# Loads by output chunk, borrowed banks and a one-level first group in the opening of a two-layer recurrent kernel

## The chip, the cores and the metric

The kernel runs on one core of one Trainium2 chip. The metric is the device time of one execution in microseconds (us), taken as the median of several runs. Beside the times there is a profile of one execution. TensorE (PE) does the matmuls, VectorE (DVE), ScalarE (ACT) and GpSimd (POOL) the elementwise work. SyncE (SP) and ScalarE issue most of the DMAs; each engine works its instructions off strictly in the order in which the program gives them.

## The reference, cut to what matters

There are 128 sequences of 128 steps with 512 features, all in float32, and two recurrent layers one behind the other, each with a residual sum.

```python
def _L0_cond_ref(h_t, z, W, b, alpha):
    Wh = W[:, :D]
    Wz = W[:, D:]
    leak = 1.0 - alpha
    def step(h, z_t):
        gate = jax.nn.sigmoid(h @ Wh.T + z_t @ Wz.T + b)
        h_new = jnp.tanh(h * leak + gate * z_t)
        return (h_new, h_new)
    ...
def _L1_cond_ref(x, h0, Wx, Wh, b):
    xw = jnp.einsum('ntd,dh->nth', x, Wx) + b
    def step(prev_h, xw_t):
        next_h = jnp.tanh(xw_t + prev_h @ Wh)
        return (next_h, next_h)
    ...
x = x + _L0_cond_ref(cond_1024, x, ...)
x = x + _L1_cond_ref(x, cond_1024, ...)
```

Per layer and step there are two 512x512 products: of the input, which does not depend on the state, and of the state, which does. Both layers start from cond.

## The kernel before

Features lie on the 128 partitions, in four chunks (C = 4), and the 128 sequences along the free dimension. A 512x512 weight is a 4x4 arrangement of 128x128 blocks, so a *state product* (`state_product`, L437) is 16 matmuls of 128 columns: two halves of eight, each with its own PSUM bank, `r0a` and `r1a` for layer 0, `r0b` and `r1b` for layer 1.

**Groups and products.** Four steps (G = 4) form a group, held in a tile T of the `ring`. Instead of 64 block products per group, the input side is computed by a scheme of seven products numbered 1 to 7, in the order 1, 2, 6, 5, 7, 3, 4 (`OUTER`), of sums of inputs and differences of weights (`wc`). `multiply` has two forms. With *one level* (L345) a product is four matmuls of 256 columns; only layer 0's group 1 uses it. With *two levels* (L351) each of the seven is split once more into seven matmuls of 128 columns, which need nested differences of weights (`raw`: tiles wra, wrb; `nested`: wna, wnb), more sums of inputs (tiles R and N beside S), a `gather` at the end, and a second seed (`seed_second`, L430) for each bank. The products accumulate in two sets of PSUM banks, A and B; ACT copies three of them aside (`keep`, L362), VectorE adds others (`add`, L375).

**Step.** Layer 0's group 0 gets its input side directly: `input_product` (L450), 16 matmuls per step into the bank of that step. From step 4 on, ACT writes the group's result into the bank as a seed (L425). Then the state product, on ACT a sigmoid (`gate0`, L478), on VectorE the mix (`mix0`, L484 and L487), on ACT a tanh (`tanh0`, L492), and on POOL the residual sum (L496). The bank of a step is free for the next step once the mix has read it. Layer 1 (`tanh1`, L505) runs LAG = 9 steps behind, so its state products begin in step 9.

**Loads.** `load_x` loads one step of x (256 KB) in four DMAs of 64 KB, `load_w0` one half of layer 0's weight (wz or wh) in four of 256 KB, `load_w1` Wx or Wh of layer 1 likewise. The loads arrive with sequences or output features on the partitions; VectorE turns them in 32x32 blocks (`prepare_x`, `transpose_w0`), for Wx and Wh of layer 1 ACT permutes them (`permute_w1`, L206). The x tiles have five buffers. DMAs of SP and ACT share eight semaphores in turn, so a load waits on its queue until the load eight places earlier has landed.

**Order.** The order is written by hand. Each piece of work is entered in a list with a planned time (`at(time, fn, ...)`), the list is sorted, and the order of each engine follows from it. `shares(t)` says which products follow the state products of step t; `start[t]` is the planned begin of step t. These times only sort; nothing waits for a clock.

In the first steps, TensorE's order is: 24 warm-up matmuls on zeros (L172, L174), the input product of step 0, group 1's products 1, 2, 6, 5, 7, 3, state product 0, input product 1, state product 1, input product 2, state product 2, input product 3, product 4 of group 1, state product 3, and then layer 0's group 2 and layer 1's group 0 by one to three products a step, up to the end of step 8.

Of the kernel before, what the change touches and what calls it, by code (L numbers as in the profile page):

```python
# [13 lines left out]
def kernel(  # L14
# [64 lines left out]

    def cost(layer, g):  # L80
        return PRODUCT if (layer, g) == ("a", 1) else DEEP
# [3 lines left out]
    def shares(t):  # L85

        g, k = divmod(t, G)
        if t < 2 * G:
            return {
                2: [(0, 1, OUTER[6:])], 3: [(0, 2, OUTER[:2])], 4: [(0, 2, OUTER[2:4])],  # L90
                5: [(0, 2, OUTER[4:6])], 6: [(0, 2, OUTER[6:]), (1, 0, OUTER[:1])], 7: [(1, 0, OUTER[1:4])],
            }.get(t, [])
        if g == NG - 1:
            said = (
                [(1, g - 2, OUTER[4:])], [(1, g - 1, OUTER[:2])],
                [(1, g - 1, OUTER[2:4])], [(1, g - 1, OUTER[4:])],
            )[k]
        elif t >= T:
            said = [(1, NG - 1, ((1,), (2, 6), (5,), (3,), (7,), (4,))[t - T])] if t < T + 6 else []
        else:  # L100
            said = (
                [(1, g - 2, OUTER[4:])], [(0, g + 1, OUTER[:4])],
                [(0, g + 1, OUTER[4:])], [(1, g - 1, OUTER[:4])],
            )[k]
        return [x for x in said if 0 <= x[1] < NG]

    start, clock = [], 26.0
    for t in range(T + LAG + 4):
        start.append(clock)
        layers = (t < T) + (t >= LAG)  # L110
        busy = STATE * layers + (STATE + 0.6 if t < G - 1 else 0.0)
        for layer, g, which in shares(t):
            busy += cost("ab"[layer], g) * len(which)
        clock += max(busy, STATE + (3.0 if t < T else 0.7))
# [20 lines left out]
    def load_w0(h, name):  # L135
        view = w0.rearrange("(a i) (h q r) -> h q i a r", i=S, h=2, q=Q)[h]
        tile_ = tpool.tile([P, C, G, P], F32, tag="T", name=f"{name}_in")
        w_in[name] = tile_.rearrange("p a m r -> p (a m) r")
        for q in range(Q):
            both[q % 2].dma_start(out=w_in[name][q * S : (q + 1) * S], in_=view[q])  # L140
# [16 lines left out]
    def load_small():  # L157
        nc.gpsimd.memset(condT, 0.0)
        nc.gpsimd.memset(rows, 0.0)
        for i, v in enumerate((b0, alpha, b1)):  # L160
            nc.gpsimd.dma_start(
                out=rows[: Q * C, i], in_=v.rearrange("(a j) -> a j", j=S)
            )
        cond_view = cond.rearrange("(a i) (q r) -> q i a r", i=S, q=Q)
        for q in range(Q):
            nc.gpsimd.dma_start(out=cond_in[q * S : (q + 1) * S], in_=cond_view[q])

    def warm_up():

        ps = [L1.state_bank(-1, half) for half in range(2)]  # L170
        for n in range(12):
            nc.tensor.matmul(ps[n % 2][:, 0, : P // 2], condT[:, n % C], condT[:, 0, : P // 2], start=True, stop=True)  # L172
        for n in range(12):
            nc.tensor.matmul(  # L174
                ps[n % 2].rearrange("p m b -> p (m b)"), condT[:, 0], condT[:, 0:2].rearrange("p c b -> p (c b)"),
                start=True, stop=True,
            )
# [21 lines left out]
    def transpose_w0(w_T, name, kc):  # L199
        nc.vector.transpose(  # L200
            w_T[:, kc].rearrange("p m (q i) -> p m q i", i=S),
            w_in[name].rearrange("p (q m) (c j) -> p c m q j", q=Q, j=S)[:, kc],
        )
# [45 lines left out]
    class Layer:  # L249
# [87 lines left out]
        def multiply(self, g, outer, tag, first):  # L337
            if first:
                sets[tag] = psum.tile([P, 8, P], F32, tag=tag, name=f"{tag}_{self.name}_{g}_{outer}")
            if (self.name, g) == ("a", 1):  # L340
                ps = sets[tag][:, 0:4].rearrange("p (m h) b -> p m (h b)", m=2)
                a, w = self.left(g, outer), self.right(outer)
                for m in range(2):
                    for c in range(2):
                        nc.tensor.matmul(  # L345
                            ps[:, m], w[:, c, m, :], a[:, c],
                            start=first and m == 0 and c == 0, stop=c == 1, skip_group_check=True,
                        )
                return
# [6 lines left out]
        def places(self, g):  # L356
            return slice(0, 4 if (self.name, g) == ("a", 1) else 7)
# [49 lines left out]
        def terms(self, t, half):  # L407
# [3 lines left out]
            if (self.name, g) == ("a", 1):  # L411
                return (c[:, k % H : 4 : H],)
# [4 lines left out]
        def state_bank(self, t, half):  # L417
            self.state[t, half] = psum.tile(
                [P, 2, P], F32, tag=f"r{half}{self.name}", name=f"r{half}{self.name}_{t}"
            )  # L420
            return self.state[t, half]
# [20 lines left out]
        def input_product(self, t):  # L442

            g, k = divmod(t, G)
            ps = [self.state_bank(t, half) for half in range(2)]
            order = [(c, m) for c in range(C) for m in range(C)]
            if t > 0:
                order.sort(key=lambda p: (p[1] // 2, p[0], p[1]))
            for c, m in order:
                nc.tensor.matmul(  # L450
                    ps[m // 2][:, m % 2], self.w[:, c, m, :], ring[g][:, c, k],
                    start=c == 0 and m % 2 == 0, stop=False, skip_group_check=True,
                )
# [60 lines left out]
    at(0.1, load_w0, 1, "wz")  # L514
    at(0.11, warm_up)
    at(0.2, load_x, 0, both)
    for n, t in enumerate((4, 5, 6, 7)):
        at(0.3 + 0.01 * n, load_x, t, (both[t % 2],))
    at(0.4, load_w0, 0, "wh0")
    at(0.5, load_x, 1)  # L520
    at(12.5, small_vectors)
    at(9.5, prepare_x, 0)
    at(9.51, load_x, 2)
    for kc in range(C):
        at(10.0 + 0.6 * kc, transpose_w0, L0.w, "wz", kc)
    at(11.9, L0.input_product, 0)
    for t, time in ((4, 12.6), (5, 13.3), (6, 14.7), (7, 15.4)):
        at(time, prepare_x, t)
    for i, time in ((5, 14.0), (6, 16.1), (7, 16.8), (4, 17.5)):
        at(time, L0.combine_weights, i, nc.vector)  # L530
    for i, time in ((5, 16.2), (6, 17.4), (3, 18.7), (7, 20.0)):
        at(time, L0.add_up, 1, i, nc.gpsimd)
    L0.products(1, OUTER[:1], 14.4)
    L0.products(1, OUTER[1:6], 17.4)
    at(18.2, from_natural, condT, cond_in)
    for kc in range(C):
        at(18.9 + 0.6 * kc, transpose_w0, L0.wh, "wh0", kc)
    at(start[0] + 1.0, prepare_x, 1)
    at(start[0] + 1.01, load_x, 3)
    at(start[0] + 1.02, load_w1, wx1, "wx")  # L540
    at(start[0] + 1.03, load_w1, wh1, "wh1")
    at(start[1] + 0.05, prepare_x, 2)
    at(start[2] + 0.05, prepare_x, 3)
    for kc in range(C):
        at(start[1] + 2.5 + 0.1 * kc, permute_w1, L1.w, "wx", kc)
        at(start[5] + 0.1 + 0.4 * kc, permute_w1, L1.wh, "wh1", kc)
    for n, i in enumerate((5, 6, 7, 4)):
        at(start[0] + 5.1 + 0.01 * n, L0.combine_raw, i, nc.vector)
        at(start[0] + n, L0.combine_nested, i, nc.gpsimd)
        at(start[1] + 3.0 + n, L1.combine_weights, i, nc.gpsimd)  # L550
        at(start[3] + 5.6 + 0.01 * n, L1.combine_nested, i, nc.gpsimd)
        at(start[3] + 5.7 + 0.01 * n, L1.combine_raw, i, nc.gpsimd)

    for n, i in enumerate((5, 6, 3, 7)):
        at(start[2] + 2.0 + 0.1 * n, L0.add_up, 2, i, nc.gpsimd)
        at(start[2] + 6.0 + 0.01 * n, L0.add_up_raw, 2, 0, i, nc.vector)
        at(start[3] + (2.6, 2.61, 4.4, 4.41)[n], L0.add_up_nested, 2, "56", i, nc.vector)
        at(start[4] + 4.4 + 0.1 * n, L0.add_up_nested, 2, "73", i, nc.vector)
        at(start[2] + 6.1 + 0.01 * n, L0.add_up_raw, 2, 1, i, nc.vector)
        at(start[5] + 5.7 + 0.01 * n, L1.add_up, 0, i, nc.gpsimd)  # L560
        at(start[6] + (2.6, 2.61, 4.4, 4.41)[n] - 0.2, L1.add_up_raw, 0, 0, i, nc.vector)
        at(start[7] + (2.6, 2.61, 4.4, 4.41)[n], L1.add_up_nested, 0, "56", i, nc.vector)
        at(start[8] + 0.1 + 0.1 * n, L1.add_up_nested, 0, "73", i, nc.vector)
        at(start[8] + (2.9, 2.91, 4.9, 4.91)[n], L1.add_up_raw, 0, 1, i, nc.vector)
# [11 lines left out]
    for t in range(T + LAG):  # L576
        g, k = divmod(t, G)
        now = start[t]
        if AHEAD <= t + AHEAD < T:
            at((now, start[0] + 0.1, start[0] + 3.0, start[1] + 1.5)[t] if t < G else now + 0.01, load_x, t + AHEAD)  # L580
        if t < T:
            for i in range(2):
# [5 lines left out]
                if G <= t + 1 < T:  # L588
                    at(end + 1.85, L0.seed, t + 1, i)
                    at(now + 6.5, L0.seed_second, t + 1, i)  # L590
            at(end + 1.8, residual, t, h0)
            now += STATE
        if t < G - 1:
            at(now + 0.6, L0.input_product, t + 1)
# [27 lines left out]
        if t < G:  # L622
            at((start[1] + 0.1, start[1] + 0.2, start[2] + 0.1, start[2] + 0.2)[t], prepare_x, t + AHEAD)
        elif t + AHEAD < T:
            at(start[t + 1] + 6.4, prepare_x, t + AHEAD)
        if k == G - 1 and 2 <= g + 1 < NG:
            at(start[t] - 0.9, L0.gather, g + 1, 0, nc.vector)
            at(start[t + 1] - 0.9, L0.gather, g + 1, 1, nc.vector)
        if k == 1 and 0 <= g - 2 < NG - 2:
# [54 lines left out]
```

## Time and profile before

| | |
|---|---|
| median of 3 runs | 1656.34 us (1655.55 to 1657.14) |
| profiled execution, its own time | 1655.27 us |
| its span | 1653.3 us |
| mean granted TensorE clock | 0.998 |
| DMA moved | 73.99 MB, mean 45 GB/s |

In the page's 40 equal slices of the span, the share of the 16 DMA engines is 0.8 in the first, 0.2 in the second and at most 0.3 after that; VectorE is at 0.5 in the first, 0.6 in the second and 0.7 to 0.8 from then on until the last.

Lines of the profile begin with a time from the span's start where they are of a timeline, then the duration, engine, line of the source, operation, output tile <- input tiles, shape and count. A bracket gives the idle time before it and what ended it. A matmul of float32 appears as two records, so "x16" of 128x128 is eight matmuls. A matmul's duration includes a part that overlaps the next, so its price in a row of them is the distance from start to start. PE is the matmul, PEld the weight load.

### The profile page before, as it was taken

How to read it: one execution, taken by the hardware profiler on the slowest of the kernel's cores; microseconds unless marked ns; L12 is line 12 of the kernel's file. 1: busy time of each engine (PE TensorE's matmuls, PEld its weight loads, DVE VectorE, ACT ScalarE, POOL GpSimd, SP SyncE). 2: the span in 40 equal slices, each digit the busy share in tenths (PEclk: the TensorE clock that was granted, in tenths of full speed). 3: DMA queues.
4: the chain of work that ended last, by engine and by line, in shares of the span. 5: the costliest groups of instructions: out<-in, count | busy, mean ns of one | idle time of the engine just before them, and what ended most of it. 6: DMA issues, size and time to landing. Idle time of an engine off the chain costs nothing.

```text
span 1653.3 us, 37130 instructions
## 1 busy us (share of the span) xinstructions
PE 1638.3 (99%) x14500; PEld 1631.6 (99%) x14500; DVE 1324.0 (80%) x2978; ACT 793.4 (48%) x2046; POOL 665.7 (40%) x540
## 2 busy tenths in 40 slices
PE   9999999999999999999999999999999999999998
PEld 8989999999999999999999999999999999999998
DVE  5688788888888887888888888888888888888784
ACT  1444454544554444545445544445454454444454
POOL 4633443343344334334433433343344334333442
PEclk9999999999999999999999999999999999999999
DMA  8201211121122112111211211121112111211113
GB/s 171 53 9 40 46 45 40 40 49 42 39 46 46 40 40 47 44 40 41 50 40 39 46 46 40 39 48 43 40 42 49 39 40 44 48 39 27 27 21 64
DMA packets 153231, 73.99 MB, mean 45 GB/s; under 512 B 16801, under 2 KB 151969, under 8 KB 153057
## 3 DMA queue, kind: packets, MB, share of 16 engines
q1 hardware_dynamic: 148992, 69.53, 19.0%
q10 hardware_dynamic: 3840, 1.84, 0.6%
q8 instruction: 113, 1.85, 0.5%
q14 instruction: 62, 0.50, 0.1%
q0 software_dynamic: 224, 0.27, 0.1%
HBM read 38.02 MB, written 33.55 MB: 43 GB/s over the span
## 4 chain that ended last, share of the span: by engine, by line
PE 93%; DVE 2%; DMA 1%; POOL 1%; ACT 1%; issue 1%; SPq 0%; ACTq 0%; DVEq 0%; POOLq 0%
PE r0b L437 13%; PE r0a L437 13%; PE r1b L437 13%; PE r1a L437 13%; PE B_b L351 12%; PE A_a L351 11%; PE A_b L351 9%; PE B_a L351 8%; DMA x<-in_x_dram 1%; POOL T L496 0%; DVE h L487 0%; PE A_a L345 0%; POOL S_a L226 0%; POOL wcb L236 0%; DVE cb L375 0%
## 5 line engine op out<-in xcount | busy, mean ns | idle before, releaser
L496 POOL TENSOR_TENSOR T<-T,h 128x512 f32<-128x512 f32 x255 | 325.4, 1276 | 956.2 <-ACT h L492 888.9
L437 PE MATMUL r0a<-h,wha 128*128 128x128 f32 x2032 | 247.9, 275 | 0.0
L437 PE MATMUL r0b<-h,whb 128*128 128x128 f32 x2032 | 247.9, 275 | 0.0
L437 PE MATMUL r1a<-h,wha 128*128 128x128 f32 x2032 | 247.7, 275 | 0.0
L437 PE MATMUL r1b<-h,whb 128*128 128x128 f32 x2032 | 247.7, 275 | 0.0
L492 ACT ACTIVATE h<-h 128x256 f32<-128x256 f32 x256 | 106.7, 417 | 278.6 <-DVE h L487 273.0
L437 PEld LDWEIGHTS r0a<-h,wha 128*128 128x128 f32 x2032 | 237.3, 192 | 0.2 <-ACT h L492 0.2
L437 PEld LDWEIGHTS r0b<-h,whb 128*128 128x128 f32 x2032 | 237.1, 192 | 0.1
L437 PEld LDWEIGHTS r1a<-h,wha 128*128 128x128 f32 x2032 | 237.1, 192 | 0.0
L437 PEld LDWEIGHTS r1b<-h,whb 128*128 128x128 f32 x2032 | 237.1, 192 | 0.0
L478 ACT ACTIVATE r0a<-r0a,per_feature 128x128 f32<-128x128 f32 x256 | 87.6, 342 | 105.1 <-PE r0a L437 101.0
L484 DVE TENSOR_TENSOR r0a<-r0a,T 128x256 f32<-128x256 f32 x128 | 54.9, 429 | 89.7 <-ACT r0a L478 89.7
L484 DVE TENSOR_TENSOR r1a<-r1a,T 128x256 f32<-128x256 f32 x128 | 55.3, 432 | 65.6 <-ACT r1a L478 65.6
L189 DVE STREAM_TRANSPOSE T<-x 128x512 f32<-128x512 f32 x128 | 86.7, 681 | 12.7 <-DMA x<-in_x_dram 11.7
L194 DVE STREAM_TRANSPOSE o<-T 128x512 f32<-128x512 f32 x128 | 90.2, 705 | 4.1 <-POOL T L496 3.6
L478 ACT ACTIVATE r1a<-r1a,per_feature 128x128 f32<-128x128 f32 x256 | 85.3, 333 | 4.2
L226 POOL TENSOR_TENSOR S_a<-T 128x512 f32<-128x512 f32 x62 | 79.9, 1289 | 14.0 <-DVE T L189 14.0
L505 ACT ACTIVATE h<-r1b,per_feature 128x128 f32<-128x128 f32 x256 | 80.8, 370 | 8.5 <-PE r1b L437 6.3
L505 ACT ACTIVATE h<-r0b,per_feature 128x128 f32<-128x128 f32 x256 | 78.1, 355 | 11.2 <-PE r0b L437 10.3
L226 POOL TENSOR_TENSOR S_b<-T 128x512 f32<-128x512 f32 x64 | 82.5, 1289 | 0.1
L487 DVE SCALAR_TENSOR_TENSOR h<-h,leak,r0a 128x128 f32<-128x128 f32 x254 | 77.0, 345 | 5.3
L487 DVE SCALAR_TENSOR_TENSOR h<-h,leak,r1a 128x128 f32<-128x128 f32 x254 | 77.0, 345 | 4.5
(204 smaller groups left out, 3712.9 us busy)
## 6 DMA issues: line engine op xcount, KB each, us to landing
out_dram<-o SPq DMA_DIRECT2D x510, 64.0 KB, 1.8
x<-in_x_dram SPq DMA_DIRECT2D x502, 64.0 KB, 2.5
wx_in<-in_L_cond_Wx_dram SPq DMA_DIRECT2D x4, 256.0 KB, 5.3
wh_in<-in_L_cond_Wh_dram SPq DMA_DIRECT2D x4, 256.0 KB, 8.3
x<-in_x_dram ACTq DMA_DIRECT2D x10, 64.0 KB, 3.9
wz_in<-in_L_cond_W_dram ACTq DMA_DIRECT2D x2, 256.0 KB, 6.2
wz_in<-in_L_cond_W_dram SPq DMA_DIRECT2D x2, 256.0 KB, 5.6
wh_in<-in_L_cond_W_dram ACTq DMA_DIRECT2D x2, 256.0 KB, 5.9
```

Source lines behind the costliest of these rows:

```text
L189: nc.vector.transpose(dst.rearrange("p c (a i) -> p c a i", i=S), src.rearrange("p a (c j) -> p c a j", j=S))
L194: nc.vector.transpose(dst.rearrange("p a (c j) -> p c a j", j=S), src.rearrange("p c (a i) -> p c a i", i=S))
L226: eng.tensor_tensor(out(which), one(), two(), op)
L351: nc.tensor.matmul(sets[tag][:, n], self.right(outer, i), self.left(g, outer, i), start=first and n % 4 == 0, stop=True, skip_group_check= ...
L437: nc.tensor.matmul(ps[:, m], self.wh[:, c, 2 * half + m, :], h[t - 1][:, c], start=alone and n == 0, stop=c == C - 1, skip_group_check=True,)
L478: nc.scalar.activation(gate[:, m], gate[:, m], AF.Sigmoid, bias=per_feature[:, 0, f : f + 1])
L484: nc.vector.tensor_tensor(gate, gate, at_of(t)[:, two[i]], ALU.mult)
L487: nc.vector.scalar_tensor_tensor(h0[t][:, f], h0[t - 1][:, f], leak[:, f : f + 1], gate[:, m], ALU.mult, ALU.add)
L492: nc.scalar.activation(h0[t][:, two[i]], h0[t][:, two[i]], AF.Tanh)
L496: (eng or nc.gpsimd).tensor_tensor(at_of(t)[:, part], at_of(t)[:, part], h[t][:, part], ALU.add)
L505: nc.scalar.activation(h1[t][:, f], ps[:, m], AF.Tanh, bias=per_feature[:, 2, f : f + 1])
```

## The change

- `FLAT`: layer 1's group 0 also goes by one level, so it has no R and N sums, no second seeds and no gather.
- `load_w0` can load by output chunk: wz comes as four chunks of four 64 KB DMAs, and is turned in eight half-size transposes (per input chunk, first output half, then second).
- The loads are in the order x_0, wz by chunk, x_1, x_4, x_5, x_6, x_7, wh, cond, x_2, x_3, x_8 to x_11, Wx, Wh; up to cond all go on SP and ACT alternately. cond leaves POOL's queue.
- `input_product` is entered by halves. Steps 1 and 3 of layer 0 use layer 1's banks (`r0b`, `r1b`). Input product 1 follows input product 0; input product 2 stands after state product 0 and product 4 of group 1; input product 3 after state product 1.
- `shares` gives product 4 of group 1 to step 0 and two products each to steps 2 to 8.
- Ten wide warm-up matmuls (256 columns) instead of twelve of 64 and twelve of 256 columns.
- Group 1's first two sums move from POOL to VectorE, the small vectors move behind wh and cond, layer 0's raw differences before the first mix. x_3 and x_8 to x_11 are turned between the mixes of steps 0 and 1, followed by the first two sums of group 2. Layer 1's raw and nested differences come later on POOL; the copies of Wx and Wh come later on ACT.

From about step 10 on, the instructions of each engine are the same in both programs. Cut to its core:

```diff
+    FLAT = ("a", 1), ("b", 0)
+
     def cost(layer, g):
-        return PRODUCT if (layer, g) == ("a", 1) else DEEP
+        return PRODUCT if (layer, g) in FLAT else DEEP
...
-        if t < 2 * G:
+        if t <= 2 * G:
             return {
-                2: [(0, 1, OUTER[6:])], 3: [(0, 2, OUTER[:2])], 4: [(0, 2, OUTER[2:4])],
-                5: [(0, 2, OUTER[4:6])], 6: [(0, 2, OUTER[6:]), (1, 0, OUTER[:1])], 7: [(1, 0, OUTER[1:4])],
+                0: [(0, 1, OUTER[6:])], 2: [(0, 2, OUTER[:2])], 3: [(0, 2, OUTER[2:4])], 4: [(0, 2, OUTER[4:6])],
+                5: [(0, 2, OUTER[6:]), (1, 0, OUTER[:1])], 6: [(1, 0, OUTER[1:3])], 7: [(1, 0, OUTER[3:5])],
+                8: [(1, 0, OUTER[5:])],
             }.get(t, [])
...
-    def load_w0(h, name):
+    def load_w0(h, name, chunks=None):
...
+        for m in (None,) if chunks is None else chunks:
+            rows_ = slice(None) if m is None else slice(m, None, C)
+            for q in range(Q):
+                both[q % 2].dma_start(out=w_in[name][q * S : (q + 1) * S, rows_], in_=view[q][:, rows_])
...
+    def load_cond():
         cond_view = cond.rearrange("(a i) (q r) -> q i a r", i=S, q=Q)
         for q in range(Q):
-            nc.gpsimd.dma_start(out=cond_in[q * S : (q + 1) * S], in_=cond_view[q])
+            both[q % 2].dma_start(out=cond_in[q * S : (q + 1) * S], in_=cond_view[q])
...
-        for n in range(12):
-            nc.tensor.matmul(ps[n % 2][:, 0, : P // 2], condT[:, n % C], condT[:, 0, : P // 2], start=True, stop=True)
-        for n in range(12):
+        for n in range(10):
...
         def state_bank(self, t, half):
...
+            tag = "b" if self.name == "a" and t in (1, 3) else self.name
+            self.state[t, half] = psum.tile([P, 2, P], F32, tag=f"r{half}{tag}", name=f"r{half}{self.name}_{t}")
...
-        def input_product(self, t):
+        def input_product(self, t, half):
...
     at(0.0, load_small)
-    at(0.1, load_w0, 1, "wz")
-    at(0.11, warm_up)
-    at(0.2, load_x, 0, both)
-    for n, t in enumerate((4, 5, 6, 7)):
-        at(0.3 + 0.01 * n, load_x, t, (both[t % 2],))
-    at(0.4, load_w0, 0, "wh0")
-    at(0.5, load_x, 1)
-    at(12.5, small_vectors)
-    at(9.5, prepare_x, 0)
-    at(9.51, load_x, 2)
+    at(0.01, warm_up)
+    at(0.1, load_x, 0, both)
+    at(0.2, load_w0, 1, "wz", range(C))
+    for n, t in enumerate((1, 4, 5, 6)):
+        at(0.4 + 0.1 * n, load_x, t, both)
+    at(3.6, prepare_x, 0)
+    at(3.7, load_x, 7, both)
+    at(3.8, load_w0, 0, "wh0")
+    at(4.0, load_cond)
     for kc in range(C):
-        at(10.0 + 0.6 * kc, transpose_w0, L0.w, "wz", kc)
-    at(11.9, L0.input_product, 0)
+        at(6.0 + 0.4 * kc, transpose_w0, L0.w, "wz", kc, two[0])
+        at(8.6 + 0.4 * kc, transpose_w0, L0.w, "wz", kc, two[1])
+    at(7.7, L0.input_product, 0, 0)
+    at(9.9, L0.input_product, 0, 1)
+    at(10.3, prepare_x, 1)
+    at(10.31, load_x, 2)
+    at(11.8, L0.input_product, 1, 0)
+    at(13.6, L0.input_product, 1, 1)
...
-    for i, time in ((5, 16.2), (6, 17.4), (3, 18.7), (7, 20.0)):
-        at(time, L0.add_up, 1, i, nc.gpsimd)
-    L0.products(1, OUTER[:1], 14.4)
-    L0.products(1, OUTER[1:6], 17.4)
-    at(18.2, from_natural, condT, cond_in)
+    for i, time, eng in ((5, 16.5, nc.vector), (6, 17.2, nc.vector), (3, 17.9, nc.gpsimd), (7, 18.0, nc.gpsimd)):
+        at(time, L0.add_up, 1, i, eng)
+    L0.products(1, OUTER[:6], 15.4)
     for kc in range(C):
-        at(18.9 + 0.6 * kc, transpose_w0, L0.wh, "wh0", kc)
+        at(20.5 + 0.6 * kc, transpose_w0, L0.wh, "wh0", kc)
+    at(23.0, from_natural, condT, cond_in)
+    at(23.01, small_vectors)
+    for half in range(2):
+        at(start[0] + STATE + PRODUCT + 0.1 + 1.8 * half, L0.input_product, 2, half)
+        at(start[1] + STATE + 0.1 + 1.8 * half, L0.input_product, 3, half)
+    at(start[0] - 1.0, prepare_x, 2)
+    at(start[0] + 5.5, prepare_x, 3)
+    at(start[0] - 0.5, load_w1, wx1, "wx")
+    at(start[0] + 8.8, load_w1, wh1, "wh1")
...
-        at(start[0] + 5.1 + 0.01 * n, L0.combine_raw, i, nc.vector)
+        at(start[0] + 0.2 + 0.01 * n, L0.combine_raw, i, nc.vector)
...
-        at(start[5] + 5.7 + 0.01 * n, L1.add_up, 0, i, nc.gpsimd)
-        at(start[6] + (2.6, 2.61, 4.4, 4.41)[n] - 0.2, L1.add_up_raw, 0, 0, i, nc.vector)
-        at(start[7] + (2.6, 2.61, 4.4, 4.41)[n], L1.add_up_nested, 0, "56", i, nc.vector)
-        at(start[8] + 0.1 + 0.1 * n, L1.add_up_nested, 0, "73", i, nc.vector)
-        at(start[8] + (2.9, 2.91, 4.9, 4.91)[n], L1.add_up_raw, 0, 1, i, nc.vector)
+        at(start[0] + 9.6 + 0.1 * n, L0.add_up, 2, i, (nc.vector, nc.gpsimd)[n // 2])
...
+        at(start[4] + 4.4 + 0.01 * n, L1.add_up, 0, i, nc.gpsimd)
...
-        if t < G - 1:
-            at(now + 0.6, L0.input_product, t + 1)
+        if t == 1:
             now += STATE
...
-            at((start[1] + 0.1, start[1] + 0.2, start[2] + 0.1, start[2] + 0.2)[t], prepare_x, t + AHEAD)
+            at(start[0] + (6.2, 6.9, 8.0, 9.5)[t], prepare_x, t + AHEAD)
...
-        if k == 1 and 0 <= g - 2 < NG - 2:
+        if k == 1 and 1 <= g - 2 < NG - 2:
```

## The prediction

> **What bounds the kernel now.** I read the page first: busy times and the chain that ended last.
>
> ```profile
> PE 1638.3 (99%) x14500; PEld 1631.6 (99%) x14500; DVE 1324.0 (80%) x2978; ACT 793.4 (48%) x2046; POOL 665.7 (40%) x540
> PE 93%; DVE 2%; DMA 1%; POOL 1%; ACT 1%; issue 1%; SPq 0%; ACTq 0%; DVEq 0%; POOLq 0%
> ```
>
> TensorE is the bound, so only matmul work added or removed, and TensorE's idle or half-speed time, can move the end. Next, the table by stage, cut where TensorE starts its first real product (13.25), step 0 (31.18), group 2's first product (61.23), layer 1's first product (83.12), step 9 (105.78) and step 10 (120.68). Columns: length, then busy time of PE, PEld, DVE, ACT, POOL, then granted clock, DMA share, GB/s.
>
> ```profile
> 0.00:13.25 13.25, 11.92 (x49) 10.87 (x49) 2.59 (x5) 0.00 (x0) 4.67 (x13) 1.00 0.93 160
> 13.25:31.18 17.93, 15.89 (x82) 13.79 (x81) 12.81 (x22) 4.32 (x5) 10.99 (x8) 0.90 0.74 157
> 31.18:61.23 30.05, 28.32 (x233) 26.97 (x232) 18.77 (x45) 9.54 (x25) 13.84 (x11) 1.00 0.62 135
> 61.23:83.12 21.89, 21.89 (x196) 21.73 (x195) 15.09 (x34) 13.61 (x35) 16.76 (x18) 1.00 0.05 13
> 83.12:105.78 22.66, 19.67 (x164) 18.61 (x163) 19.65 (x44) 9.83 (x23) 7.17 (x6) 1.00 0.05 13
> 105.78:120.68 14.90, 13.91 (x123) 13.56 (x122) 13.38 (x28) 7.56 (x19) 7.08 (x6) 1.00 0.01 1
> 120.68:1653.00 1532.32, 1526.66 (x13666) 1526.08 (x13664) 1241.72 (x2806) 748.53 (x1940) 605.22 (x480) 1.00 0.19 42
> ```
>
> The last row has nothing to gain, and from about step 10 on the two programs have the same instructions. The prediction is therefore about when TensorE reaches step 9, 105.78 now. TensorE's timeline gives the prices and the stall:
>
> ```profile
> 9.17 0.79 PE L174 MATMUL r1b_-1_112<-condT 128*128 128x256 f32 x2
> 9.80 0.59 PE L174 MATMUL r0b_-1_111<-condT 128*128 128x256 f32 x2
> 16.82 1.89 PE L345 MATMUL A_a<-T,wa 128*128 128x256 f32 x8
> 18.55 1.89 PE L345 MATMUL B_a<-T,wa 128*128 128x256 f32 x8
> 22.48 3.10 PE L345 MATMUL A_a<-S_a,wca 128*128 128x256 f32 x8 [2.04 <-POOL S_a L226]
> 25.37 2.51 PE L345 MATMUL B_a<-S_a,wca 128*128 128x256 f32 x8
> ```
>
> From start to start a one-level product takes 1.73 us (16.82 to 18.55), a state or input product 3.57 (16 pairs), a two-level product 1.56 (61.23 to 62.79). Product 6 of group 1 waits 2.04 us for POOL's sums, and then products run at half clock: 22.48 to 31.18 is 8.70 for 4 x 1.73 = 6.92.
>
> Lost time per stage (length less work): 13.25 to 31.18, 17.93 - (3.57 + 6 x 1.73) = 4.0; to 61.23, 30.05 - (7 x 3.57 + 1.73 for steps 0 to 3, three input products and product 4) = 3.3; to 83.12, 21.89 - (7 x 1.56 + 3 x 3.57) = 0.3; to 105.78, 22.66 - (7 x 1.56 + 2 x 3.57) = 4.6; to 120.68, 14.90 - (2 x 3.57 + 4 x 1.56) = 1.5. The waits of TensorE (total, times, longest) name part of it:
>
> ```profile
> PE B_b L351 <- DVE R_b L226: 1.6, 2, 0.9
> PE r0b L437 <- DVE r0b L430: 0.9, 1, 0.9
> PE B_b L351 <- DVE cb L375: 0.7, 1, 0.7
> PE r1a L450 <- DVE h L487: 0.9, 2, 0.7
> ```
>
> Layer 1's two-level group 0 waits for its sums (R_b), its additions (cb) and its second seeds; the input products of steps 1 to 3 wait until the mix (h) frees their bank.
>
> **The loads.** Now x_7 lands at about 17.7 (VectorE turns it and x_6 from 17.75). The changed program needs x_0, wz, x_1, x_4 to x_7 by then: 40 loads of 64 KB, 2.62 MB. The nearest rows are two stages with both queues loading, 2:10 and 10:15, and one with SP alone (same columns):
>
> ```profile
> 2.00:10.00 8.00, 8.00 (x32) 7.35 (x32) 0.00 (x0) 0.00 (x0) 3.51 (x7) 1.00 1.15 199
> 10.00:15.00 5.00, 5.00 (x32) 4.60 (x31) 4.22 (x12) 0.00 (x0) 0.00 (x0) 1.00 0.80 161
> 46.00:54.00 8.00, 7.64 (x64) 7.26 (x64) 3.81 (x10) 2.04 (x6) 7.84 (x7) 1.00 0.51 131
> ```
>
> From 2 us on, 199 GB/s puts x_7 at 15.2, 161 at 18.3, 131 at 22.0. 161 is the row of 64 KB loads that wait for earlier ones, as all will now; 64 KB landed in 2.3 to 3.6 us there, and eight in flight per 2.9 us are 180. I take 17.4.
>
> The Trainium skill (DMA: Bandwidth & Descriptors, Bandwidth) speaks against cutting wz's four loads into sixteen: it gives 64 KB transfers 138 GB/s against 341 for 1 MB, and asks for big batches. By it, as an estimate, x_7 would land at 21.0 and 3.6 us of the gain below would go. The first row above, 199 GB/s with a third of its bytes in 64 KB loads, disagrees.
>
> **Start of the real work.** Ten wide warm-up matmuls replace 24 mixed ones. Wide pairs took 0.96 us until about 9.4 and 0.43 after (timeline): the faster clock came 8.1 us after the first matmul and 2.9 after the first wide one. Starting at 1.33, the ten end at 7.2 if 2.9 counts and 10.1 if 8.1 does; all are wide, so I take the earlier end, 7 to 8. At eight loads per 2.9 us, x_0 in by 3.6, wz's first two chunks are in at 6.5 and the last two at 9.5; VectorE's eight half-size transposes (0.34 each by the 0.67 row) let step 0's input product end at 11.4. x_1 (in at 11, turned by 11.7) lets step 1's input product run 11.7 to 15.3, in layer 1's banks. Before, that product stood after step 0. Products 1 and 2, which need x_4 and x_5 (turned by 14.6), follow to 18.8. An end of the warm-up at 10.1 would cost 1.
>
> **Product 6.** After x_7: transpose 0.68, and the two sums that move from POOL (1.6 each) to VectorE (0.65 each, POOL idle) end at 19.4. ACT has the cond loads ahead of its table load (1.28) and the copy of product 1 (0.59), so ends at 19.7. Product 6 starts at 19.75 instead of 22.48. POOL's other two sums (3.2) end at 22.7, before product 7 at 23.2. Four products at full clock: step 0 could start at 26.7, before 31.18.
>
> **VectorE up to the first mix** is the new tight place. From 19.4: two weight differences beside POOL's sums (1.75 each) 22.9; an addition 23.5; four wh transposes 26.0; cond 26.7 (so step 0 starts 26.75); the small vectors, moved here, 1.1; addition, x_2, addition 2.0; layer 0's eight raw differences 2.2 to 3.3; then the first mix, 1.05: done at 33.2. TensorE does step 0 to 30.3 and product 4 to 32.05, then step 2's input product waits 1.15 for its bank. Step 1 runs to 40.35, step 3's input product waits 0.15, step 2 ends at 47.6. The cond loads leave POOL's queue, idle until 19.15 (four issues of 0.56), for SP and ACT behind wh; in flight with it four such loads took 6.3 to 6.9 us, so cond is in by 24.4, 1.6 before VectorE wants it; past that, step 0 loses one for one. VectorE's transposes of x_3, x_8 to x_11 and two sums (4.5) stand ahead of step 1's mix, needed at 39.4; x_11, last of six tiles at SP's 1.9 us each from 22.5, lands near 36 and must by 37.4.
>
> Shorter stalls than 2.04 us left the clock at 1.00, so I keep it there; if this one grows to 2, the half clock costs 1.8 more. The skill (TensorE: Matmul & The Clock Gate, Why this matters for your kernels) allows gaps up to about 3 us; by it nothing would be charged. The 2.04 us row contradicts it.
>
> **Steps 3 to 8.** Work from 47.6: six steps 21.42, group 2 10.92, layer 1's group 0 by one level 7 x 1.73 = 12.11 (1.2 more than now): 92.05. One level takes from VectorE 16 sums (7.9 us), eight second seeds (3.4), two gathers (4.1) and 0.4 of each of three additions, so most of the 4.6 lost there should go. A step with two products gives the chain gate 0.75, mix 1.05, tanh 0.45 some 3.1 us of cover; the 61.23 row shows that this loses 0.3. Wx's copies move past step 2's tanh on ACT, POOL's four combinations (5.1) follow; layer 1 needs them near 75, some 15 us later; past that TensorE waits. Wh1 moves too, needed after 95.
>
> I add 0.6 for hand-overs, 0.3 for group 2, 0.7 for layer 1's group: step 9 at 93.65. That is 12.1 earlier. Of step 9's loss of 1.5, its layer-1 seed wait (0.9) goes: 13.1. The waits list named only half of the 3.3 lost between 31 and 61, so I charge 1.3 for such unnamed time: 11.8. Profiled 1655.27 us (span 1653.3 plus 2.0 around it) becomes 1643.5; the median of the runs is 1.07 above that profile: 1644.5.
>
> **Rivals.** *Late loads or a late VectorE.* At 131 GB/s x_7 lands at 22.0, 4.6 later, and all follows: gain 7.2, 1649. Or the raw differences take 3.3 and the wait passes 2 us: 1.1 plus 1.8 less, 1647.5. For it: VectorE has hardly an idle us from 17.4 to 33; against: 131 is one queue's rate. *One level does not cure layer 1's stall.* If POOL's sums or the copies were behind it, 3.9 stays lost: 1648.5. Against: three of the four waits name VectorE. *Slower:* x_11. Step 1's mix queues behind its transpose, so TensorE loses one for one from a landing at 37.4; at 49.2 the whole gain is gone, and one at 53 gives 1660. SP is in order and now waits long for buffers; but that holds x_12, and Wx and Wh1, which delayed x_10 and x_11 now, stand behind it in the changed program.
>
> **How the numbers follow.** Forecast 0.64, its own range 1641 to 1647 (x_7 between 15.2 and 18.3, unnamed time 0 to 3). Late loads or VectorE 0.17; one level without effect 0.08; x_11 late 0.11, of which 0.07 ends slower and 0.04 within 0.2% of now. A difference of 0.2% (3.3 us) is about what a measurement of this kernel can tell from none. Faster: 0.64 + 0.17 + 0.08 = 0.89. The range 1641 to 1650 leaves out the x_11 case and the tails.
>
> **What would show it.** Right: product 6 near 19.8, step 0 near 26.8, a wait of about 1.2 for h at step 2's input product, clock 1.00 from 20 to 30, step 9 near 94, no wait for R_b. Wrong: x_7 turned after 20; a half clock after 30; TensorE waiting over 3 us in step 1; step 9 after 102.

## The result and the profile after

The changed kernel takes 1642.80 us (median of four runs, 1642.41 to 1643.46) against 1656.74 for the kernel before in the same set (1655.55 to 1657.32): a ratio of 0.9917, 95% interval 0.9900 to 0.9934. The forecast was 1644.5 with a range of 1641 to 1650. The profiled execution took 1643.46 us, of which the span is 1641.7; the forecast for it was 1643.5. A second set of runs, on the chip of the last experiment, gave 1643.14 against 1657.14 (0.9914, 0.9899 to 0.9928).

The medians differ by 13.9 us, the two profiled spans by 11.6. The profiled execution of before (1653.3) was shorter than all 31 others whose span is on record (1653.4 to 1656.1), that of after the longest of eight (1640.6 to 1641.7). The tables explain the 11.6; what the other executions of before lost beyond it was not traced.

The page of the kernel after, busy times and the chain that ended last:

```profile
PE 1630.9 (99%) x14430; PEld 1624.0 (99%) x14430; DVE 1316.4 (80%) x2958; ACT 792.1 (48%) x2046; POOL 658.6 (40%) x532
PE 94%; DMA 2%; DVE 2%; issue 1%; ACT 1%; SPq 0%; POOL 0%; ACTq 0%; DVEq 0%; POOLq 0%
```

TensorE is as full as before, and the chain still runs through it; transfers have 2% of the chain, with 1% before. The table by stage of the kernel after has its cuts at the first real product (8.38), step 0 (29.09), group 2's first product (49.87), layer 1's first product (71.86), step 9 (94.95) and step 10 (109.26). The columns are those of the table before.

```profile
0.00:8.38 8.38, 7.05 (x20) 5.77 (x21) 2.04 (x5) 0.00 (x0) 2.45 (x9) 1.00 0.57 147
8.38:29.09 20.71, 18.27 (x113) 16.18 (x112) 15.01 (x28) 3.79 (x5) 8.05 (x6) 1.00 0.75 163
29.09:49.87 20.78, 20.43 (x170) 19.53 (x169) 17.34 (x42) 5.87 (x16) 5.41 (x5) 1.00 0.80 173
49.87:71.86 21.99, 21.93 (x197) 21.73 (x195) 15.14 (x32) 14.10 (x35) 14.30 (x11) 1.00 0.14 37
71.86:94.95 23.09, 22.97 (x154) 21.17 (x152) 14.92 (x35) 12.60 (x35) 9.94 (x8) 1.00 0.09 24
94.95:109.26 14.31, 13.74 (x121) 13.58 (x122) 10.79 (x22) 7.00 (x19) 9.23 (x9) 1.00 0.01 2
109.26:1641.60 1532.34, 1526.47 (x13666) 1526.00 (x13664) 1241.15 (x2801) 748.76 (x1940) 609.25 (x487) 1.00 0.19 42
```

The last row is the control: 1532.34 us against 1532.32 before. (POOL has 487 instructions there instead of 480, because layer 1's raw differences now end behind step 10; TensorE does not feel it.) Everything was won ahead of step 10, which comes at 109.26 instead of 120.68. Lost time per stage, by the same prices: 8.38 to 29.09, 20.71 - (2 x 3.57 + 6 x 1.73) = 3.2; 29.09 to 49.87, 20.78 - (5 x 3.57 + 1.73) = 1.2; 71.86 to 94.95, 23.09 - (7 x 1.73 + 3 x 3.57) = 0.3, where the kernel before lost 4.6; step 9, 14.31 - (2 x 3.57 + 4 x 1.56) = 0.9, where it lost 1.5. The clock column stands at 1.00 in every row; before, it fell to 0.90 in the second.

TensorE's timeline of the kernel after:

```profile
6.61 0.64 PE L181 MATMUL r0b_-1_102<-condT 128*128 128x256 f32 x2
8.38 1.95 PE L455 MATMUL r0a<-T,wa 128*128 128x128 f32 x16
...
21.02 1.97 PE L352 MATMUL A_a<-S_a,wca 128*128 128x256 f32 x8 [1.02 <-DVE S_a L233]
23.81 1.99 PE L352 MATMUL B_a<-S_a,wca 128*128 128x256 f32 x8 [0.82 <-DVE ca L382]
...
29.09 1.95 PE L444 MATMUL r0a<-condT,wha 128*128 128x128 f32 x16
...
34.40 1.98 PE L455 MATMUL r0a<-T,wa 128*128 128x128 f32 x16
```

Product 6 starts at 21.02, after a wait of 1.02 for VectorE's sums. Product 5 waits too, 0.82 for an addition (`ca`), and step 0 begins at 29.09. Step 2's input product (34.40) follows product 4 with no wait listed. All waits that the profile lists for TensorE after the start and up to step 10:

```profile
PE A_a L352 <- DVE S_a L233: 1.0, 1, 1.0
PE B_a L352 <- DVE ca L382: 0.8, 1, 0.8
PE r1a L455 <- DVE wa L207: 0.6, 1, 0.6
PE A_a L358 <- POOL T L501: 0.6, 1, 0.6
```

Neither R_b, N_b, cb nor the second seeds (r0b) are left. The last line is in step 9. VectorE's timeline shows why the first two are there:

```profile
16.02 0.71 DVE L196 STREAM_TRANSPOSE T<-x 128x512 f32<-128x512 f32 x1 [0.47 <-DMA x<-in_x_dram]
18.72 0.71 DVE L196 STREAM_TRANSPOSE T<-x 128x512 f32<-128x512 f32 x1 [1.98 <-DMA x<-in_x_dram]
...
21.40 1.75 DVE L243 TENSOR_TENSOR wca<-wa,wca 128x512 f32<-128x512 f32 x1
23.08 0.68 DVE L382 TENSOR_TENSOR ca<-B_a,ka_p 128x512 f32<-128x512 f32 x1
```

VectorE turned x_6 at 16.02, then stood idle for 1.98 us until x_7 was there and turned it at 18.72. The addition that product 5 needs then queues behind two weight differences, the second of which took 1.75 beside POOL.

### The profile page after: what moved, and what is told of

The parts are those of the page before. It is cut to its first block, busy times and chain, and to the rows that moved or that the text cites. A ratio compares the mean times of both kernels' runs of the same rounds, so it can differ in the third digit from the quotient of the medians.

```text
span 1641.7 us, 36995 instructions
## 1 busy us (share of the span) xinstructions
PE 1630.9 (99%) x14430; PEld 1624.0 (99%) x14430; DVE 1316.4 (80%) x2958; ACT 792.1 (48%) x2046; POOL 658.6 (40%) x532
## 4 chain that ended last, share of the span: by engine, by line
PE 94%; DMA 2%; DVE 2%; issue 1%; ACT 1%; SPq 0%; POOL 0%; ACTq 0%; DVEq 0%; POOLq 0%
PE r0a L444 13%; PE r0b L444 13%; PE r1b L444 13%; PE r1a L444 13%; PE B_b L358 12%; PE A_a L358 11%; PE A_b L358 9%; PE B_a L358 8%; DMA x<-in_x_dram 1%; DMA wh_in<-in_L_cond_W_dram 1%; DVE h L492 0%; DMA wz_in<-in_L_cond_W_dram 0%; POOL T L501 0%; PE r1a L455 0%; SPq L128 0%
## 5 line engine op out<-in xcount | busy, mean ns | idle before, releaser
L386 ACT COPY ca<-A_a 128x896 f32<-128x896 f32 (+1 forms) x31 | 27.8, 896 | 101.5 <-PE A_a L358 101.5
```

The source lines that it names most:

```text
L386: nc.scalar.copy(self.part(g, 1, 0)[:, n], sets[tag][:, n])
```

## The experiments

Ten kernels ran, in three sets; each set has its own runs of the kernel before (1656.66, 1657.35 and 1657.14), so kernels of different sets are compared by their ratios, or by where their traces stand. Code cuts show the core of each edit; "..." marks what is left out. "Step 9" is the start of its state product on TensorE.

| kernel | median us | ratio to before (95%) | step 0 | step 9 | span |
|---|---|---|---|---|---|
| before | 1656.74 | 1 | 31.18 | 105.78 | 1653.3 |
| after | 1642.80 | 0.9917 (0.9900 to 0.9934) | 29.09 | 94.95 | 1641.7 |
| one level alone | 1650.98 | 0.9964 (0.9952 to 0.9977) | 31.17 | 102.35 | 1648.4 |
| two levels again | 1654.46 | 0.9988 (0.9979 to 0.9997) | 28.66 | 103.69 | 1652.4 |
| own banks | 1646.83 | 0.9943 (0.9930 to 0.9957) | 28.63 | 98.23 | 1645.0 |
| old warm-up | 1645.46 | 0.9933 (0.9920 to 0.9945) | 31.29 | 96.73 | 1643.5 |
| wz whole | 1644.90 | 0.9925 (0.9912 to 0.9937) | 30.39 | 95.84 | 1643.4 |
| no x_7 | 1642.54 | 0.9913 (0.9899 to 0.9926) | 28.27 | 93.72 | 1640.7 |
| sums on POOL | 1644.33 | 0.9925 (0.9913 to 0.9938) | 32.66 | 98.10 | 1644.8 |
| spread | 1643.00 | 0.9916 (0.9902 to 0.9929) | 28.11 | 94.11 | 1640.9 |
| after, again | 1643.14 | 0.9914 (0.9899 to 0.9928) | 28.94 | 94.79 | 1641.6 |
| addition first | 1642.68 | 0.9912 (0.9896 to 0.9929) | 28.06 | 94.19 | 1641.0 |

**One level alone**: the kernel before, with layer 1's group 0 by one level and nothing else.

```diff
-            if (self.name, g) == ("a", 1):
+            if (self.name, g) in FLAT:          # FLAT = ("a", 1), ("b", 0); likewise in cost, places, terms
...
-        at(start[6] + (2.6, 2.61, 4.4, 4.41)[n] - 0.2, L1.add_up_raw, 0, 0, i, nc.vector)
...
-        if k == 1 and 0 <= g - 2 < NG - 2:
+        if k == 1 and 1 <= g - 2 < NG - 2:
```

> The kernel before, with layer 1's group 0 by one level and nothing else of the change. If the sums and second seeds on VectorE were what TensorE waited for, the stage of layer 1's products (83.12 to 105.78 before, 4.6 us lost) loses about 0.6, its work grows by 1.2, and the seed wait of 0.9 in step 9 goes: some 3.7 us faster than before. If POOL or the copies were behind the waits, they stay and only the work of 1.2 us is added: slower by 1.2.

The span is 4.9 shorter, the median 5.7. Layer 1's first product starts where it did (83.11 against 83.12). Cut there, at step 9 and at step 10, the table of this kernel reads:

```profile
83.11:102.35 19.24, 19.24 (x123) 17.74 (x121) 14.20 (x30) 9.27 (x25) 7.19 (x6) 1.00 0.06 15
102.35:115.75 13.40, 13.40 (x122) 13.40 (x121) 9.77 (x21) 7.00 (x18) 6.70 (x6) 1.00 0.01 2
```

The first stage's work is 7 x 1.73 + 2 x 3.57 = 19.25, step 9's is 13.38. TensorE loses nothing in either, where it lost 4.6 and 1.5; 6.1 less lost for 1.2 more work is the 4.9, more than the 3.7 expected. The rival, that POOL's sums or ACT's copies are behind the stall, is excluded: both kept their places here. (POOL's nested and raw weight differences, which one level does not need, had ended at 75.8 before, well ahead of 83.) Its opening matters below: product 6 waits 2.0 us as before.

**Two levels again**: the changed kernel, with layer 1's group 0 back on two levels. VectorE's extra sums get places between the steps that now carry the products, and POOL's differences come earlier.

```diff
-    FLAT = ("a", 1), ("b", 0)
+    FLAT = (("a", 1),)
...
-        at(start[6] + 6.0 + 0.01 * n, L1.combine_nested, i, nc.gpsimd)
-        at(start[10] + 1.0 + 0.01 * n, L1.combine_raw, i, nc.gpsimd)
+        at(start[5] + 4.5 + 0.01 * n, L1.combine_nested, i, nc.gpsimd)
+        at(start[4] + 4.5 + 0.01 * n, L1.combine_raw, i, nc.gpsimd)
...
+        at(start[4] + 5.5 + 0.01 * n, L1.add_up_raw, 0, 0, i, nc.vector)
+        at(start[5] + 5.5 + 0.01 * n, L1.add_up_nested, 0, "56", i, nc.vector)
+        at(start[6] + 5.5 + 0.01 * n, L1.add_up_nested, 0, "73", i, nc.vector)
+        at(start[7] + 5.5 + 0.01 * n, L1.add_up_raw, 0, 1, i, nc.vector)
...
```

> The changed kernel with layer 1's group 0 back on two levels; its sums stand on VectorE between the mixes and layer 1's raw and nested differences come before its products, as before. If one level is worth what the forecast says, the stage of layer 1's products loses 2 to 4 us more, less 1.2 of work, and the seed wait of step 9 comes back: 2 to 3.7 us slower than the changed kernel. If it was the even spread of two products per step that removed the waits, it is 1.2 us faster.

Far more than either: step 9 comes 8.7 later than after and step 10 10.5 later (119.79), and nearly all of the change's gain is gone. TensorE's longest wait in the whole opening:

```profile
PE r0a L444 <- DVE r0a L437: 4.9, 2, 4.2
```

It is a second seed of layer 0, in step 8 (94.03 on VectorE), which stands there behind the previous step's mix and then four sums for layer 1 (91.89 to 94.11, one of them 1.37 us beside POOL, the others 0.28). After the 4.2 the clock fell: the stretch 90 to 100 has it at 0.83. So VectorE's queue is the mechanism, and a schedule with two products a step has less room for two levels than the old one. Layer 1's seed wait in step 9 is back too, with 2.0. How much of the 8.7 is due to the places I chose for the sums is open; the table of *one level alone* is the cleaner price.

**Own banks**: the changed kernel, with steps 1 and 3 back in layer 0's banks, so that each input product comes behind the previous step.

```diff
...
-            tag = "b" if self.name == "a" and t in (1, 3) else self.name
+            tag = self.name
...
-    at(11.8, L0.input_product, 1, 0)
-    at(13.6, L0.input_product, 1, 1)
...
-        at(start[0] + STATE + PRODUCT + 0.1 + 1.8 * half, L0.input_product, 2, half)
-        at(start[1] + STATE + 0.1 + 1.8 * half, L0.input_product, 3, half)
+        at(start[0] + STATE + PRODUCT + 0.1 + 1.8 * half, L0.input_product, 1, half)
+        at(start[1] + STATE + 0.1 + 1.8 * half, L0.input_product, 2, half)
+        at(start[2] + STATE + 0.1 + 1.8 * half, L0.input_product, 3, half)
...
```

> The changed kernel with the input products of steps 1 and 3 in layer 0's own banks, so each stands after the state product of the step before, as in the kernel before. If the borrowed banks fill the time in which the loads are waited for, step 0 begins no earlier than 29.1 although 3.57 us of work have left its front, and the bank waits return: 3.6 plus about 1 us, 4.6 slower than the changed kernel. If the loads alone carry the gain, no difference beyond 0.5.

Step 9 is 3.3 later than after, the ratio 0.26% higher (about 4.3 us). TensorE's timeline of this kernel at product 1:

```profile
15.27 3.50 PE L352 MATMUL A_a<-T,wa 128*128 128x256 f32 x8 [2.28 <-DVE T L196]
```

Without input product 1 there, TensorE waits 2.28 for x_5 and then runs at half clock (product 2 follows 3.30 later instead of 1.73). Step 0 starts 0.46 earlier than after, but 3.57 of work that was done before it is still to do: 3.57 - 0.46 = 3.1 of the 3.3. So the borrowed banks are worth not the short waits for the mix (0.2 each here) but work for TensorE in a stretch in which it has to wait for loads.

**Old warm-up**: the changed kernel with the old 24 warm-up matmuls.

```diff
-        for n in range(10):
+        for n in range(12):
+            nc.tensor.matmul(ps[n % 2][:, 0, : P // 2], condT[:, n % C], condT[:, 0, : P // 2], start=True, stop=True)
+        for n in range(12):
```

> The changed kernel with the 24 warm-up matmuls of before. The first real product starts near 13.3 instead of 8.4, the products before x_7 end at 23.9, product 6 starts there instead of at 21.0, product 5's wait of 0.8 goes: step 0 begins 1.7 us later and the kernel is 1.7 slower than the changed one. If the loads hide the start, no difference; if the whole 4.9 count, 4.9 slower.

Step 9 is 1.78 later, the span 1.8, the ratio 0.16% (2.7 us). The first real product starts at 13.78 instead of 8.38: of 5.4 us only 1.8 reach step 9, because TensorE then meets x_7 with no wait at all. Those 5.4 us were cover for the loads.

**wz whole**: the changed kernel with wz in four loads of 256 KB.

```diff
-    at(0.2, load_w0, 1, "wz", range(C))
+    at(0.2, load_w0, 1, "wz")
```

> The changed kernel with wz in four loads of 256 KB instead of sixteen of 64 KB, in the same place. If the bytes set the landing, x_7 is turned at the same time (18.7) within half a us, and only the first product, which now waits for all of wz, starts later: 0 to 1 us slower than the changed kernel. If small loads cost rate, as the skill's figures say (an estimate of 3.6 us), x_7 is turned 2 to 3 us earlier and the kernel is 1 to 1.5 faster.

From VectorE's timeline of this kernel, the line that answers to 18.72 above:

```profile
18.71 0.71 DVE L196 STREAM_TRANSPOSE T<-x 128x512 f32<-128x512 f32 x1 [1.63 <-DMA x<-in_x_dram]
```

Within 0.01 of the changed kernel; in the other kernels with the same loads x_7 was turned between 18.21 and 18.82, so how wz is cut makes no difference to x_7 beyond this scatter. What the chunks bring is the start. Here wz landed a median of 6.6 us (SP) and 7.3 us (ACT) after its issue (3.0 and 3.1 for the chunks), TensorE waited 3.96 for it and started at 11.27 with its first eight matmuls at half clock (3.40 from start to start instead of 1.79), and step 9 came 0.9 later. The Trainium skill (DMA: Bandwidth & Descriptors, Bandwidth) gives small transfers a fraction of the bandwidth of big ones; its table is of transfers issued from GpSimd, while SP and ACT issue them here, and with eight loads in flight the loss it would mean does not show.

**No x_7**: the changed kernel without the load of x_7; step 7 takes x_6's data instead, so part of the input is left out.

```diff
+        if t == 6:
+            x_in[7] = x_in[6]
...
-    at(3.7, load_x, 7, both)
```

> The changed kernel without the load of x_7; step 7 takes the data of x_6. If the landing of x_7 sets product 6, ACT's table load and the loads behind it, product 6 starts near 19.9 instead of 21.0 and step 0 begins 1.2 to 2 us earlier: 1.2 to 2 us faster than the changed kernel. If VectorE's work up to the first mix sets the pace whatever the loads do, the gain is below 0.5.

A miss in size. Step 9 is 1.23 earlier and the span 1.0 shorter, the ratio lower by 0.04%, within its interval. x_6 and its copy are turned only at 17.30:

```profile
17.30 1.30 DVE L196 STREAM_TRANSPOSE T<-x 128x512 f32<-128x512 f32 x2 [1.85 <-DMA x<-in_x_dram]
```

So product 6 (20.20) still waits 0.5, and product 5 keeps its 0.8. Taking away 256 KB moved the sums by 0.8 us, because x_6, turned at 16.02 in the changed kernel, is itself 1.3 later here. Why is taken up under x_7 below.

**Sums on POOL**: the changed kernel with group 1's first two sums back on POOL.

```diff
-    for i, time, eng in ((5, 16.5, nc.vector), (6, 17.2, nc.vector), (3, 17.9, nc.gpsimd), (7, 18.0, nc.gpsimd)):
+    for i, time, eng in ((5, 16.5, nc.gpsimd), (6, 17.2, nc.gpsimd), (3, 17.9, nc.gpsimd), (7, 18.0, nc.gpsimd)):
```

> The changed kernel with group 1's first two sums back on POOL (1.64 us each there, 0.69 on VectorE). If the sums are on the path, product 6 starts 1.9 us later, less product 5's wait of 0.8, which loses its cause: 1.1 to 1.9 us slower than the changed kernel. If the path runs through wh, cond and VectorE, no difference beyond 0.5.

The median ratio is 0.08% higher (1.3 us), inside what was expected with the sums on the path but too small for the intervals to tell from none. The profiled execution was the longest of its five (1646.62; 1643.33 to 1645.56 for the others), and its TensorE timeline shows what that one met:

```profile
22.72 3.78 PE L352 MATMUL A_a<-S_a,wca 128*128 128x256 f32 x8 [3.08 <-POOL S_a L233]
26.29 3.08 PE L352 MATMUL B_a<-S_a,wca 128*128 128x256 f32 x8
```

A wait of 3.08 for the sums, and then two products at 3.57 and 2.91 from start to start instead of 1.73. Step 0 is 3.6 later than after: 1.7 from the product's later start, 3.0 from the half clock, less 0.8 for product 5's wait, which is gone, and 0.2 of hand-over around it. The other four executions left no trace.

**Spread**, an attempt to beat the changed kernel: the addition ahead of one weight difference, the raw differences half before step 0's mix and half before step 1's, POOL's nested ones later.

```diff
-    for i, time in ((5, 11.0), (6, 14.0), (7, 18.0), (4, 18.7)):
+    for i, time in ((5, 11.0), (6, 14.0), (7, 18.95), (4, 23.005)):
...
-        at(start[0] + 0.2 + 0.01 * n, L0.combine_raw, i, nc.vector)
-        at(start[0] - 5 + n, L0.combine_nested, i, nc.gpsimd)
+        at(start[n // 2] + 3.0 + 0.01 * n, L0.combine_raw, i, nc.vector)
+        at(start[0] - 2.5 + 0.1 * n, L0.combine_nested, i, nc.gpsimd)
```

> An attempt to beat the changed kernel: the addition that product 5 waits for stands ahead of the last two weight differences, the fourth difference behind cond, layer 0's raw differences half between the mixes of step 0 and half between those of step 1, the nested ones on POOL later. If VectorE's queue up to the first mix is the bound, product 5's wait of 0.8 goes and step 2's input product follows product 4 at once, and the kernel is 1.1 to 1.8 us faster than the changed one. If x_11's landing (36.1) or the mix of step 1 is late next, less than 0.5.

The trace gains 0.8 at step 9, the ratio (0.9916) is that of the changed kernel. Product 5's wait is gone, but product 6's grew to 1.5, and step 3's input product waits 0.6 for the mix, which now has raw differences ahead of it.

**Addition first**, with the changed kernel run again beside it: only the addition moves ahead of the last two weight differences.

```diff
-    for i, time in ((5, 11.0), (6, 14.0), (7, 18.0), (4, 18.7)):
+    for i, time in ((5, 11.0), (6, 14.0), (7, 18.95), (4, 18.96)):
```

> The changed kernel itself once more, on the same chip as the next run, so that differences of one or two us need not be taken over two sets of runs of before. Both theories: the ratio to before is 0.9917 within its interval of 0.9900 to 0.9934, step 9 at 94.95 within 0.5, product 6 waits about 1.0 and product 5 about 0.8.

> The changed kernel with the addition that frees product 5's bank put ahead of the last two weight differences on VectorE; nothing else moves. Theory, the wait of product 5 is VectorE's queue: the addition ends at about 21.5 instead of 23.7, the wait of 0.82 is gone, step 0 starts near 28.3 instead of 29.09 (its other condition, cond, is turned at 27.3 and product 3 ends then), and step 9 comes 0.8 earlier: 0.8 us faster. Rival, the time there is covered further on: VectorE's queue up to the first mix has the same length, so the mix is done at 34.2 as before and step 2's input product, at TensorE at 33.6, waits 0.6 for it: 0.2 us faster or nothing.

The repeat came as expected: step 9 at 94.79, waits of 0.93 and 0.82. TensorE's timeline of *addition first*:

```profile
21.08 1.97 PE L352 MATMUL A_a<-S_a,wca 128*128 128x256 f32 x8 [1.37 <-DVE S_a L233]
22.88 1.89 PE L352 MATMUL B_a<-S_a,wca 128*128 128x256 f32 x8
```

Product 5 follows product 6 without its wait, so VectorE's queue was the cause. Step 0 starts at 28.06 (28.94 in the changed kernel beside it) and step 9 at 94.19 (94.79): 0.88 became 0.60 on the way, since step 2's input product is now 0.2 behind the end of product 4 (31.63 + 1.73 to 33.57). The spans differ by 0.6 and the medians by 0.46, below what the measurement resolves. Theory and rival each had a part: most of the wait comes back, the mix takes the rest. No version measurably beats the changed kernel.

## Why the prediction was right, and where it was not

**The sum.** The forecast for step 9 was 93.65 plus 1.3 of unnamed time, 94.95; it was 94.95. That is partly luck. Step 0 came 2.34 later than forecast (29.09 for 26.75), steps 0 to 2 took what was forecast (20.78 for 20.85), and from there to step 9 TensorE lost 0.6 (45.08 for 44.45 of work) where 0.3, 0.7 and 0.6 were charged. 93.65 + 2.34 - 0.07 - 1.0 = 94.92. The allowance for unnamed time paid for two errors with names. The forecast of the median was 1.7 too high for another reason: it added 1.07 to the profiled time, because before's median lay that far above its profile; after's median lies 0.66 below its own (1642.80, 1643.46). And 12.1 plus 0.9 is 13.0, not the 13.1 written there.

**The signs.** Of those named for right, a clock of 1.00 from 20 to 30, step 9 near 94 and no wait for R_b came. Product 6 near 19.8, step 0 near 26.8 and a wait of 1.2 at step 2's input product did not: 21.02, 29.09, and 0.3 on its second half. Of those named for wrong none came.

**x_7, a term mis-sized.** Landing was put at 17.4, between the 16.6 that 180 GB/s gives and the 18.3 of 161, and the transpose followed at 18.72. The rates held, as three stretches of the kernel after show (columns of the table by stage):

```profile
2.00:10.00 8.00, 8.00 (x35) 6.81 (x34) 2.14 (x5) 0.00 (x0) 1.30 (x3) 1.00 0.74 191
10.00:15.00 5.00, 4.40 (x39) 4.21 (x39) 4.03 (x9) 0.00 (x0) 0.00 (x0) 1.00 0.71 180
15.00:22.00 7.00, 5.98 (x35) 5.14 (x35) 4.49 (x7) 1.87 (x2) 1.04 (x1) 1.00 1.03 187
```

The bytes were too few: from 2 to 18.7 these rates make 8 x 191 + 5 x 180 + 3.7 x 187 = 3.1 MB, of which only 2.6 are the 40 loads that were counted. About 0.5 MB belong to wh, whose loads were issued from 14.3 on and shared the engines with x_7's last pieces, issued by 14.1; these took up to 4.4 us to land, where 2.9 was the median. This is worked out from the trace, and no run took wh away. *No x_7* supports it: there wh's loads stand right behind x_6's (issued from 13.3), x_6's last two took 4.0 and 4.4, and x_6 is turned 1.3 later although the same loads stand ahead of it. The tile that stands right ahead of wh comes late.

Product 6 came 1.27 later than forecast, as x_7 did. But its other condition was as late: ACT's copy of product 1, forecast to end at 19.7, ended at 20.78, behind a table load and the cond loads that ACT issued until 18.87; the sums ended at 20.88. By these times, with x_7 alone on time, product 6 would have gained about 0.1. That is an estimate; no run shows it.

**Product 5, a customer overlooked.** The prediction listed VectorE's queue with the addition at 23.5, and used it only for the cond transposes behind it. Product 5 needs that addition for its bank. By the prediction's own numbers product 6 would have ended at 21.5 and product 5 waited until 23.5. It waited from 22.75 to 23.81, 1.06 in all, 0.82 of it listed. 1.27 + 1.06 is the 2.3 by which step 0 was late. *Addition first* shows the cause.

**The first mix was the tight place**, but without a price. It was forecast for 33.2 with step 2's input product waiting 1.15. It ended at 34.27 (the raw differences took 2.1, the lower end; the leak 1.06 beside POOL), 0.1 before TensorE asked, because TensorE was late by more. Only the second half of that input product lost 0.3, to the second mix (35.83 + 0.61), which waits for ACT's gate. In *addition first*, where TensorE came 0.8 earlier, 0.2 to 0.3 of it showed.

**Layer 1's stall went, by the cause that was named.** After has 0.3 lost in that stage where 0.7 was charged, and *one level alone* nothing. Its worth was undersized: 4.9 in the span alone, where 4.6 + 0.9 lost less 1.2 of work and 0.7 kept would have been 3.6.

**The start.** 8.38 for "7 to 8", at a price of nothing: in the repeated run TensorE started at 7.96 and waited 0.5 for wz. Input product 0 lost 0.6 to wz's last chunks and product 2 ended at 19.85, before x_7 was usable. Step 9's seed wait went, as forecast, but 0.6 appeared at group 3's product 6 (the trace names POOL; ACT's copy of product 1, which ran until 105.9, also ended just before it), so step 9 became 0.6 shorter, not 0.9. Which of the two was the cause no run shows.

**The rivals.** Late loads: x_7 was late by 1.3, not by 4.6. One level without effect: excluded. x_11: VectorE turned x_3 and x_8 to x_11 in one go from 36.35 to 39.4 with no wait for a load, and step 1's mix followed at 41.1, behind ACT's gate.

**Who won what.** Taken away one at a time, the warm-up costs 1.8, the chunks 0.9 and the borrowed banks 3.3 at step 9, and one level by itself gives 4.9 at step 10: 10.9, for 120.68 - 109.26 = 11.4 in all. That they add up so nearly is chance. The sums on VectorE are not in the list; the trace of *sums on POOL* puts them at 3.2 at step 9, its median at 1.3 us. The new order of the loads and cond's move to SP and ACT were never undone alone. And in the changed schedule, taking one level away costs 10.5 at step 10, not 4.9.

## What to carry to other kernels

When a queue is worked out for the engine that gets tight, write beside each instruction in it who waits for it, not only when the last one ends. A one-level scheme that does a little more work on the bound engine can win if it frees the engine that feeds it, and its price is read from the stage where the waits are. Work that needs only early data (here an input product in a borrowed bank) is worth most where the bound engine would otherwise wait for loads, because it also keeps the clock up.

## What the runs showed of the hardware

**The rise of the clock varies from run to run.** TensorE's wide warm-up pairs took 0.85 from start to start until the clock rose and 0.43 after it; the prediction's 0.96 is the first pair alone. Of the same program, one execution had the step near 6.6 (the 6.61 line above), 5.3 after the first matmul, and the other near 4.5, 3.2 after it. The prediction read 2.9 after the first wide one from a single execution; no one figure holds for both. The Trainium skill (TensorE: Matmul & The Clock Gate, What's actually happening) describes a window that runs freely and a count of slow matmuls that changes from run to run, which agrees with these two; the window itself no run shows.

**An idle of 2 us sometimes halves the clock.** In the kernel before, 2.04 us were followed by half clock, and 2.28 in *own banks*; in *one level alone*, 2.0 us at the same product were not:

```profile
PE A_a L347 <- POOL S_a L228: 2.0, 1, 2.0
```

Nor were 2.05 us in *two levels again*: the eight matmuls behind them took 2.05, those behind the 4.2 above 3.63.

```profile
109.57 2.05 PE L444 MATMUL r0b<-condT,whb 128*128 128x128 f32 x16 [2.05 <-DVE r0b L437]
```

In *one level alone*, step 0 began at 31.17, as before, although its first real product came 1.1 later (14.34): what the later start cost, the full clock gave back. After 1.48 us in *spread* and 1.02 after, nothing was lost. The allowance of about 3 us that the prediction quotes does not hold here; between 2.0 and 2.3 us the outcome varied, and the length alone does not decide it (2.04 against 2.05).

**Elementwise work beside POOL.** A 128x512 difference on VectorE took 0.65 to 0.69 alone and 1.36 to 1.76 beside POOL's sums, the leak (128x4) 1.06 instead of 0.17 in *addition first*, and POOL's own sums 1.64 instead of 1.27.
